# Layer 1's products of directly taken columns, made during layer 0, in a four-layer graph kernel

## The chip, the cores and the metric

The kernel runs on one core of a Trainium2 chip. The metric is the device time of one execution in microseconds (us). The kernel before the change took 1016.37 us (median of three runs, 1012.38 to 1018.28).

The engines are named as in the profile: PE is the matrix engine, PEld its weight loads, DVE the vector engine, ACT the scalar engine, POOL the engine that here issues the gathers by index, and SP the one that issues plain DMAs. [...]

## What is computed

There are N = 2708 nodes with D = 512 features, and a sparse weighted adjacency matrix `adj` with positive entries and a full diagonal. Four layers each replace `x` by `layernorm(x + layer(x, adj))`. The two that the change touches:

```python
# layer 0
adj_hat = adj + eye;  d = 1 / sqrt(adj_hat.sum(1))
layer0 = ((d[:, None] * adj_hat * d[None, :]) @ x) @ W.T + b
# layer 1
head = (adj > 0);  head = head / max(sqrt(sum(head * head, -1)), 1e-12)
inc  = adj + head
layer1 = (inc @ x) / sum(inc, -1)
```

Layer 1's incidence matrix depends on `adj` alone, so only its right factor, the rows of layer 0's result `x1`, has to be waited for. Layer 2 is an attention layer with gates, and layer 3 a product with signs; neither is touched.

## The kernel before

The node rows are cut into 22 blocks of 128 (block 21 has 20 rows). A prologue searches, for every block, which columns hold entries, and copies the needed pieces of the transposed adjacency into `packed[b]`: tiles of 128 columns by the block's rows. A block's tiles are of three kinds. **Direct tiles** (`direct(b)`, the table `DIRECT` at L34) are whole column blocks taken as they lie; for blocks 1 to 20 these are only column block 0, or 0 and 1, since the graph is densest there. Fifteen blocks have them: 1, 3, 5, 15 and 17 have two, ten others one, 20 tiles in all. **Gathered tiles** are 128 columns picked by a list; `ROOM` (L31) says how many, 98 over all blocks. Some of them are **narrow**: they concern only 32 or 64 of the block's rows. Block 0 is taken whole, a column block at a time.

Layer 0 (the loop at L1459) goes through the blocks in the order `sequence` = 0, 1, 21, 2, 3, ..., 20. For each block POOL issues one gather of 128 rows of `y_rows` per gathered tile (L613), PE multiplies tile by tile into a PSUM bank (L1369, in `add_tile`), DVE adds the result to the old rows (L1484), and the layer norm follows on DVE, with one square root on ACT (L642 to L683). The new rows stay in SBUF (`place_of_x(b)`) and are stored to `x1_rows` (L1488). Beside it runs `grow1` (L1421): block 0 of layer 1 needs all column blocks, and each block's part of it (two DVE operations for the incidence tile, one product on PE) is made two blocks after that block is finished. The table `between` hangs further steps on the places of the sequence: the counts and roots from which layer 1's row heads `head_row`, its scales `rdeg` and its diagonal factors `own1` come, for group n of the blocks at places 2 + 2n and 3 + 2n, and preparations of layers 2 and 3. At place 4 and after, head rows of the first group are therefore there.

Layer 1 (the loop at L1637) takes the blocks in the same order. It builds the incidence tiles on DVE (L1650, L1651), multiplies direct tiles first, then whole gathered tiles, then narrow ones (L1674, again by L1369), and in `finish1` ACT scales the block's own rows (L1562), DVE adds the scaled product (L1563), and the layer norm ends on ACT (L680). The gathers of layer 1 read `x1_rows` and so can't begin before layer 0's last rows are stored. PE also makes `project1` of the block before (four transposes L1588, a copy on ACT L1590, sixteen product records L1595) and `grow2` (L1628, L1629), the part of layer 2's block 0.

Within an engine the order of instructions isn't that of the source alone: a planner in the compiler's front end orders them by its own estimate of when each can run, and earlier source lines go first among the ready ones.

A product of a 128x128 tile by 128x512 values in float32 stands in the trace as two PE records, so "x2" is one tile.

Of the kernel before, what the change touches and what calls it, by code (L numbers as in the profile page):

```python
# [8 lines left out]
F32 = mybir.dt.float32  # L9
# [5 lines left out]
ALU = mybir.AluOpType  # L15
# [4 lines left out]
P = 128  # L20
# [487 lines left out]
def sparse_layers(ctx, tc, x, adj, adj_t, w0_t, b0, w_sa, a_sa, w_gcnb, b_gcnb, wa, ba, wb, bb, w3_t,  # L508
# [819 lines left out]
        t, spans = i - len(direct(b)), SPANS[SPLIT[b]]  # L1328
        return spans[t][1:] if 0 <= t < len(spans) else (0, rows(b))

    def whole_runs(b: int, most: int, apart: bool = False):

        nd, n = len(direct(b)), narrow(b)
        whole = [i for i in range(tiles(b)) if not nd <= i < nd + n]
        runs = []
        for i in whole:
            if runs and sum(runs[-1]) == i and runs[-1][1] < most and not (apart and i == nd + n):
                runs[-1] = (runs[-1][0], runs[-1][1] + 1)
            else:
                runs.append((i, 1))  # L1340
        return runs
# [31 lines left out]
    def last_of(b: int, i: int, order):  # L1373
# [3 lines left out]
            span(b, j)[1] <= r0 or span(b, j)[0] >= r1 for j in order[order.index(i) + 1 :]  # L1377
        )

    sum1 = ps_mm.tile([P, D], F32, tag="sum1", name="l1_0", bufs=1)  # L1380
    with tc.tile_pool(name="s_l0", bufs=10, reuse_waits="tile") as lp:


# [37 lines left out]
        def grow1(j: int):  # L1421

            r = rows(j)
            inc = lp.tile([P, P], F32, tag="inc0", name=f"inc0_{j}", bufs=2)
            a = packed[0][:r, j, :]
            nc.vector.scalar_tensor_tensor(
                inc[:r], a, 0.0, head0_row[0][:r], op0=ALU.is_gt, op1=ALU.mult
            )
            nc.vector.tensor_tensor(inc[:r], inc[:r], a, op=ALU.add)
            nc.tensor.matmul(  # L1430
                sum1, inc[:r], place_of_x(j)[:r, :D], start=(not grown1),
                stop=(len(grown1) == NB - 1),
            )
            grown1.append(j)

        between = {
            2: [attention_loads], 4: [lambda: attention_columns(0)],
# [21 lines left out]
        for at, b in enumerate(sequence):  # L1459
            m = rows(b)  # L1460
            old = place_of_x(b)
            nc.vector.tensor_tensor(old[:m, :D], old[:m, :D], b0_row[:m], op=ALU.add)
            if b:
                nd = len(direct(b))
                order_ = in_turns(b)
                src = {}
                for i in order_:
                    if i >= nd:
                        src[i] = gathered(lp, D, y_rows, b, i - nd)
                    else:  # L1470
# [12 lines left out]
            t = work.tile([P, D], F32, tag="t", name=f"t0_{b}")  # L1483
            nc.vector.scalar_tensor_tensor(  # L1484
                t[:m], ps[:m], dinv[:m, b : b + 1], old[:m, :D], op0=ALU.mult, op1=ALU.add
            )
            layernorm(old[:m, :D], t, m, f"0_{b}")
            nc.sync.dma_start(x1_rows[b * P : b * P + m, :], old[:m, :D])  # L1488
            for step_ in between.get(at, []):
                step_()  # L1490
        for b in sequence[-2:]:
            grow1(b)
    l0_ps.close()

    wp2 = w2.enter_context(tc.tile_pool(name="s_w22", bufs=1, side="right", reuse_waits="tile"))
# [62 lines left out]
    def finish1(b: int, ps):  # L1558
        m = rows(b)
        new, old = pairs.get(b, (f[b], f[b]))  # L1560
        t = work.tile([P, D], F32, tag="t", name=f"t1_{b}")
        nc.scalar.activation(t[:m], old[:m, :D], AF.Copy, scale=own1[:m, b : b + 1])  # L1562
        nc.vector.scalar_tensor_tensor(  # L1563
            t[:m], ps[:m], rdeg[:m, b : b + 1], t[:m], op0=ALU.mult, op1=ALU.add
        )
        layernorm(new[:m, :D], t, m, f"1_{b}", on_act=True)
        nc.sync.dma_start(x2_rows[b * P : b * P + m, :D], new[:m])

    with tc.tile_pool(name="s_l1", bufs=8, reuse_waits="tile") as lp:
# [67 lines left out]
        for at, b in enumerate(sequence):  # L1637
            m = rows(b)
            if b:
                nd = len(direct(b))  # L1640
                order_ = in_turns(b)
                src = {i: place_of_x(direct(b)[i]) for i in range(nd)}
                for i in order_:
                    if i >= nd:
                        src[i] = gathered(lp, D, x1_rows, b, i - nd)
                ps = ps_mm.tile([P, D], F32, tag="mm", name=f"l1_{b}")
                inc_of = {}

                def incidence(iv, a, row):
                    nc.vector.scalar_tensor_tensor(iv, a, 0.0, row, op0=ALU.is_gt, op1=ALU.mult)  # L1650
                    nc.vector.tensor_tensor(iv, iv, a, op=ALU.add)  # L1651

                for i0, n in whole_runs(b, 3):
                    inc = lp.tile([P, 3, P], F32, tag="inc0", name=f"inc{b}_{i0}", bufs=3)
                    iv = inc[:, :n, :m]
                    incidence(
# [549 lines left out]
```

## Time and profile before

| what | value |
|---|---|
| median of three runs | 1016.37 us (1012.38 to 1018.28) |
| the profiled execution's own time | 1015.66 us |
| its span, first to last instruction | 1013.9 us |
| PE busy over the span | 867.5 us (86%) |
| DVE / ACT / POOL busy | 654.6 / 381.2 / 513.0 us |
| mean granted PE clock | 0.924 |
| gathers of layer 0 (L613, y_rows) | 98, mean 995 ns |
| gathers of layer 1 (L613, x_rows) | 98, mean 967 ns |
| layer 1's direct products (L1369, `l<-f_other,inc`) | 40 records, 369.1 to 568.5 us |
| layer 0's main loop, after its first gathers | 224 to 361 us |
| change of layers | 361 to 400 us |
| layer 1, steady | 400 to 596 us |

The stage borders are read from the DVE operation that takes a block's product from PSUM: L1484 runs from 198.5 to 360.7 us, L1563 from 366.9 to 575 us. Busy time of an engine counts a record's whole length; PE's records overlap, so PE can be busy without being at its peak. "Remote" and "another core or an unknown queue" in a list of waits mean that the counter that was waited for was raised by nothing that the profile could name.

### The profile page before, as it was taken

Reading aid. Unit: us, or ns where it says so; the run is one execution under the profiler, and the core shown is the slowest. Engines: PE = TensorE matmul, PEld = TensorE weight load, DVE = VectorE, ACT = ScalarE, POOL = GpSimd, SP = SyncE. Lnnn points to the kernel's source line nnn. Section 1 sums busy time; section 2 is a strip of 40 time slices with the busy share of each in tenths; the row PEclk is TensorE's granted clock in tenths of the full one; section 3 lists DMA queues with packets and bytes.
Section 4 is the critical chain, followed back from the end, with each engine's and each line's share of the span. In section 5 each row is a group of like instructions: output and inputs, shape, how many; then the busy total and the mean of one; then the engine's idle time right before and its main releaser. Section 6 shows DMA issues by size and latency. Waiting matters only on the chain.

```text
span 1013.9 us, 12803 instructions
## 1 busy us (share of the span) xinstructions
PE 867.5 (86%) x3659; PEld 458.7 (45%) x3659; DVE 654.6 (65%) x2538; ACT 381.2 (38%) x822; POOL 513.0 (51%) x579
## 2 busy tenths in 40 slices
PE   1888889659587977989999988998999999699983
PEld 0444444212122324455555544453555555378762
DVE  5889797717366863546455436666888777556765
ACT  2665555100000012545445433333444333254654
POOL 2677888567666533646434034453454320066761
PEclk9898889879798988999999998999999999889986
DMA  9999895467676634766645266676786551299985
GB/s 288 332 330 313 293 299 162 142 197 215 189 228 202 199 122 132 216 198 207 199 150 165 80 235 239 225 272 219 261 320 224 176 176 44 82 308 331 310 233 169
DMA packets 93557, 220.06 MB, mean 217 GB/s; under 512 B 13660, under 2 KB 28364, under 8 KB 93476
## 3 DMA queue, kind: packets, MB, share of 16 engines
q0 software_dynamic: 43008, 127.61, 42.1%
q1 hardware_dynamic: 38520, 76.78, 22.3%
q10 hardware_dynamic: 11948, 14.76, 4.4%
q8 instruction: 31, 0.51, 0.2%
q14 instruction: 50, 0.41, 0.1%
HBM read 178.21 MB, written 31.71 MB: 207 GB/s over the span
## 4 chain that ended last, share of the span: by engine, by line
PE 63%; DVE 15%; issue 6%; DMA 6%; another core or an unknown queue 5%; ACT 3%; POOL 1%; ACTq 0%; DVEq 0%; SPq 0%; POOLq 0%
PE l L1369 11%; PE h L1595 7%; PE e L1820 6%; PE a L1820 6%; PE l L2075 4%; PE y L1106 4%; PE pg L1868 4%; PE l L2114 3%; PE pc L1868 3%; DMA xg<-x_rows,i 2%; PE e L1628 2%; PE px L1929 2%; PE a L1629 2%; DVE s_mask L874 1%
## 5 line engine op out<-in xcount | busy, mean ns | idle before, releaser
L613 POOL DMA_INDIRECT xg<-x_rows,i x98 | 94.8, 967 | 113.4 <-PE l L1369 65.7
L1072 POOL DMA_INDIRECT a<-in_adj_t_dram,row_at x98 | 111.0, 1132 | 59.2 <-DVE deg L817 24.0
L613 POOL DMA_INDIRECT xg<-y_rows,i x98 | 97.5, 995 | 50.3 <-issue 21.8
L1106 PE MATMUL y<-s_w,xt 128*128 128x512 f32 (+1 forms) x176 | 96.8, 702 | 0.0
L1369 PE MATMUL l<-xg,a 128*32 128x512 f32 (+3 forms) x196 | 83.2, 657 | 12.1 <-DMA xg<-y_rows,i 11.8
L613 POOL DMA_INDIRECT xg<-xw_rows,i x70 | 71.4, 1020 | 39.9 <-issue 16.5
L1796 POOL DMA_INDIRECT xg<-x_rows,i x60 | 59.9, 999 | 61.8 <-ACT ae L1551 18.0
L1595 PE MATMUL h<-s_wsa,xt 128*128 128x256 f32 (+3 forms) x352 | 83.5, 391 | 5.2 <-ACT xt L1590 5.0
L1796 POOL DMA_INDIRECT a<-x_rows,i x38 | 36.9, 970 | 93.3 <-DVE mask L1554 38.0
L1595 PEld LDWEIGHTS h<-s_wsa,xt 128*128 128x128 f32 (+1 forms) x352 | 65.4, 190 | 30.6 <-ACT xt L1590 14.0
L809 ACT ACTIVATE unused<-arow 128x1408 uint8<-128x1408 f32 (+3 forms) x44 | 58.3, 1325 | 2.4 <-DMA x_rows<-s_zero 1.7
L1106 PEld LDWEIGHTS y<-s_w,xt 128*128 128x128 f32 (+1 forms) x176 | 37.3, 223 | 43.4 <-issue 43.3
L2075 PE MATMUL l<-ws,pw 128*128 128x512 f32 (+1 forms) x210 | 52.0, 401 | 3.7 <-DVE pw L1999 3.7
L1820 PE MATMUL a<-xg,a 128*32 128x512 f32 (+2 forms) x120 | 50.9, 626 | 4.2 <-DMA xg<-x_rows,i 4.2
L1820 PE MATMUL e<-xg,ae 128*32 128x512 f32 (+2 forms) x120 | 47.9, 601 | 0.9 <-ACT ae L1556 0.9
L642 ACT ACTIVATE rsqs<-mv 128x1 f32<-128x1 f32 (+2 forms) x56 | 11.3, 201 | 94.8 <-DVE mv L671 48.9
L2075 PEld LDWEIGHTS l<-ws,pw 128*128 128x128 f32 (+1 forms) x210 | 40.4, 194 | 14.0 <-DVE pw L1999 4.6
L1868 PE MATMUL pg<-s_wg,pt 128*128 128x256 f32 (+1 forms) x176 | 44.9, 397 | 1.3 <-ACT pt L1856 1.3
L895 PE MATMUL find<-s_sides,s_mask 128*128 128x5 bf16 (+1 forms) x462 | 15.7, 166 | 34.8 <-DVE s_mask L891 25.0
L667 DVE BATCH_NORM_STATS2 st<-t 128x6 f32<-128x512 f32 (+1 forms) x66 | 45.3, 686 | 0.3
L1369 PEld LDWEIGHTS l<-xg,a 128*32 128x32 f32 (+3 forms) x196 | 19.6, 148 | 53.2 <-issue 33.0
L673 POOL TENSOR_TENSOR rs<-mv,s_neg_half 128x1 f32<-128x1 f32 (+1 forms) x22 | 12.9, 588 | 60.5 <-DVE mv L671 51.1
(306 smaller groups left out, 1965.6 us busy)
## 6 DMA issues: line engine op xcount, KB each, us to landing
arow<-in_adj_dram SPq DMA_DIRECT2D x21, 704.0 KB
arow<-in_adj_dram SPq DMA_DIRECT2D x21, 650.0 KB
x_rows<-f SPq DMA_DIRECT2D x40, 256.0 KB
aw<-in_adj_t_dram SPq DMA_DIRECT2D x21, 320.0 KB
y_rows<-yt ACTq DMA_DIRECT2D x20, 256.0 KB
x_rows<-h SPq DMA_DIRECT2D x19, 257.0 KB
f<-in_x_dram SPq DMA_DIRECT2D x19, 256.0 KB
h_own<-x_rows SPq DMA_DIRECT2D x19, 256.0 KB
```

The source lines that it names most:

```text
L613: nc.gpsimd.indirect_dma_start(out=t, out_offset=None, in_=src[:, :], in_offset=bass.IndirectOffsetOnAxis(ap=index[b][:, i : i + 1], axis=0),)
L667: nc.vector.bn_stats(st[:m], t[:m])
L809: nc.scalar.activation(unused[:m, : ar.shape[1]], ar, AF.Copy, accum_out=row_sums[:m, b, h : h + 1])
L1072: nc.gpsimd.indirect_dma_start(out=packed[b][:, t + len(direct(b)), :], out_offset=None, in_=adj_t, in_offset=bass.IndirectOffsetOnAxis(ap ...
L1106: nc.tensor.matmul(ps[:m], xt[:, k, :m], w0[:, k, :], start=(k == 0), stop=(k == KC - 1))
L1369: nc.tensor.matmul(ps[r0:r1], weights, moving, start=(i == order[0]), stop=last_of(b, i, order))
L1595: nc.tensor.matmul(ps, xt[:, k, :m], w[:, k, :], start=(k == 0), stop=(k == KC - 1))
L1796: nc.gpsimd.indirect_dma_start(out=g, out_offset=None, in_=x2_rows[:, :], in_offset=bass.IndirectOffsetOnAxis(ap=index[b][:, t : t + 1], a ...
L1820: nc.tensor.matmul(ps[r0:r1], weights, moving, start=(i == order[0]), stop=last_of(b, i, order))
L1868: nc.tensor.matmul(ps, pt[:, k, :m], w[:, k, :], start=(k == 0), stop=(k == KC - 1))
L2075: nc.tensor.matmul(whole[b], p[:r, h, b * P : (b + 1) * P], g[:r, :], start=(j == 0 and h == 0), stop=(j == NB - 1 and h == 1),)
L2114: nc.tensor.matmul(ps[:m], p[:, h, i * m : (i + 1) * m], src[i0 + i], start=False, stop=(i0 + i == len(src) - 1 and h == 1),)
```

## The change

The products of direct tiles leave layer 1's loop. A new function `begin1(b)` makes them in layer 0: two DVE operations for the incidence tiles, one product for each direct tile, ACT's scaling of the block's own rows, and one new DVE operation that adds the scaled product to them. The result stands where the block's rows of `x1` stood (`f[b]`; these have been stored by then, and block 0's product has used them). `begin1(b)` runs at the end of a place of the sequence, from two places after block b's own, and no earlier than place 4 + 2n of its group n. That puts block 1 at place 4; 2 and 3 at 6; 4 and 5 at 8; 7 at 10; 8 at 11; 9 at 12; 11 at 14; 13 at 16; 14 at 17; 15 at 18; 16 at 19; 17 at 20; and 20 after the loop. Its products use two PSUM banks in turn that are free at that time. Two small SBUF tiles of 1 KB a partition are added. Layer 1 then works only with gathered tiles, and `finish1` adds its product to what was begun.

```diff
-    def whole_runs(b: int, most: int, apart: bool = False):
+    def whole_runs(b: int, most: int, apart: bool = False, since: int = 0):
         nd, n = len(direct(b)), narrow(b)
-        whole = [i for i in range(tiles(b)) if not nd <= i < nd + n]
+        whole = [i for i in range(since, tiles(b)) if not nd <= i < nd + n]
...
+    def incidence(iv, a, row):
+        nc.vector.scalar_tensor_tensor(iv, a, 0.0, row, op0=ALU.is_gt, op1=ALU.mult)
+        nc.vector.tensor_tensor(iv, iv, a, op=ALU.add)
...
+        def begin1(b: int):
+            m, n = rows(b), len(direct(b))
+            inc = heads.tile([P, 2, P], F32, tag="incd", name=f"incd{b}", bufs=2)
+            iv = inc[:, :n, :m]
+            incidence(
+                iv, packed[b][:, :n, :],
+                head_row[:, None, b * P : b * P + m].to_broadcast([P, n, m]),
+            )
+            pool, tag = ((ps_mm, "sum0"), (ps_t, "t"))[len(begun) % 2]
+            ps = pool.tile([P, D], F32, tag=tag, name=f"l1d_{b}", bufs=1)
+            for i, j in enumerate(direct(b)):
+                nc.tensor.matmul(
+                    ps[:m], iv[:, i, :], place_of_x(j)[:, :D], start=(i == 0), stop=(i == n - 1)
+                )
+            nc.scalar.activation(
+                f[b][:m], place_of_x(b)[:m, :D], AF.Copy, scale=own1[:m, b : b + 1]
+            )
+            nc.vector.scalar_tensor_tensor(
+                f[b][:m], ps[:m], rdeg[:m, b : b + 1], f[b][:m], op0=ALU.mult, op1=ALU.add
+            )
+            begun.add(b)
+
+        to_begin = {}
+        for b in sorted(DIRECT):
+            n = GROUPS.index(group_of[b])
+            to_begin.setdefault(max(sequence.index(b) + 2, 4 + 2 * n), []).append(b)
...
             for step_ in between.get(at, []):
                 step_()
+            for c in to_begin.pop(at, []):
+                begin1(c)
         for b in sequence[-2:]:
             grow1(b)
+        for at in sorted(to_begin):
+            for c in to_begin[at]:
+                begin1(c)
...
-        nc.scalar.activation(t[:m], old[:m, :D], AF.Copy, scale=own1[:m, b : b + 1])
+        own = f[b] if b in begun else t
+        if b not in begun:
+            nc.scalar.activation(t[:m], old[:m, :D], AF.Copy, scale=own1[:m, b : b + 1])
         nc.vector.scalar_tensor_tensor(
-            t[:m], ps[:m], rdeg[:m, b : b + 1], t[:m], op0=ALU.mult, op1=ALU.add
+            t[:m], ps[:m], rdeg[:m, b : b + 1], own[:m, :D], op0=ALU.mult, op1=ALU.add
         )
...
-                order_ = in_turns(b)
-                src = {i: place_of_x(direct(b)[i]) for i in range(nd)}
-                for i in order_:
-                    if i >= nd:
-                        src[i] = gathered(lp, D, x1_rows, b, i - nd)
+                order_ = [i for i in in_turns(b) if i >= nd]
+                src = {i: gathered(lp, D, x1_rows, b, i - nd) for i in order_}
...
-                for i0, n in whole_runs(b, 3):
+                for i0, n in whole_runs(b, 3, since=nd):
```

More of the change, by code (lines that the diff above doesn't have):

```diff
@@ L1378, in last_of @@
         )
+    def incidence(iv, a, row):
+        nc.vector.scalar_tensor_tensor(iv, a, 0.0, row, op0=ALU.is_gt, op1=ALU.mult)
+        nc.vector.tensor_tensor(iv, iv, a, op=ALU.add)
     sum1 = ps_mm.tile([P, D], F32, tag="sum1", name="l1_0", bufs=1)
+    begun = set()
     with tc.tile_pool(name="s_l0", bufs=10, reuse_waits="tile") as lp:
@@ L1640, in sparse_layers @@
                 nd = len(direct(b))
-                order_ = in_turns(b)
-                src = {i: place_of_x(direct(b)[i]) for i in range(nd)}
-                for i in order_:
-                    if i >= nd:
-                        src[i] = gathered(lp, D, x1_rows, b, i - nd)
+                order_ = [i for i in in_turns(b) if i >= nd]
+                src = {i: gathered(lp, D, x1_rows, b, i - nd) for i in order_}
                 ps = ps_mm.tile([P, D], F32, tag="mm", name=f"l1_{b}")
                 inc_of = {}
-                def incidence(iv, a, row):
-                    nc.vector.scalar_tensor_tensor(iv, a, 0.0, row, op0=ALU.is_gt, op1=ALU.mult)
-                    nc.vector.tensor_tensor(iv, iv, a, op=ALU.add)
-                for i0, n in whole_runs(b, 3):
+                for i0, n in whole_runs(b, 3, since=nd):
                     inc = lp.tile([P, 3, P], F32, tag="inc0", name=f"inc{b}_{i0}", bufs=3)
```

## The prediction, made before the changed kernel was run

> **What bounds the kernel now.** The change moves work from layer 1 into layer 0, so I read first how full each engine is in each stage (the table by stretches: busy us and records of each engine, granted PE clock, DMA share).
>
> ```profile
> core 0: us, PE busy (x) PEld busy (x) DVE busy (x) ACT busy (x) POOL busy (x), PEclk, DMA share, GB/s
> 224.00:262.00 38.00, 29.68 (x91) 9.33 (x91) 22.26 (x96) 1.82 (x8) 27.34 (x27) 0.90 0.68 199
> 262.00:320.00 58.00, 44.78 (x150) 12.85 (x150) 32.40 (x144) 3.15 (x13) 38.02 (x39) 0.85 0.73 213
> 320.00:361.00 41.00, 40.06 (x131) 13.61 (x131) 35.08 (x167) 3.83 (x16) 16.99 (x17) 0.95 0.56 169
> 361.00:400.00 39.00, 27.22 (x64) 11.31 (x65) 18.46 (x74) 7.05 (x14) 16.41 (x17) 0.82 0.49 149
> 400.00:596.00 196.00, 190.19 (x725) 106.31 (x724) 99.45 (x388) 94.23 (x161) 80.25 (x83) 0.99 0.55 168
> ```
>
> Layer 1 (400 to 596) is PE's: busy 190 of 196 us, DVE and ACT half idle. But layer 0 isn't a stage with an idle PE either. Only its first part has room (PE 74.5 of 96 us up to 320); from 320 to 361 PE is busy for 40.1 of 41 us, with DVE at 35.1 close behind it. The chain of waits in that last part confirms it, with nothing but products in it:
>
> ```profile
> 346.10 0.97 PE l L1430 x2
> 347.07 1.86 PE l L1369 x4
> 348.93 1.06 PE l L1430 x2
> 349.99 2.06 PE l L1369 x4
> ```
>
> By engine, the chain's pieces add up to 39.9 us PE of 41 here; in 262 to 320 to 22.0 PE, 18.7 DVE and 12.7 "another core or an unknown queue" (DVE waiting for PE's counter); in 224 to 262 mostly to gathers and unnamed waits (PE 8.7 of 38).
>
> Last, PE's timeline in layer 1, for what a direct product costs there and what stands around it:
>
> ```profile
> 473.31 0.66 PE L1588 MATMUL xt1p<-s_ident,f 128*128 128x128 f32 x4
> 473.81 1.02 PE L1369 MATMUL l<-xg,inc 128*128 128x512 f32 x2
> 474.67 3.73 PE L1595 MATMUL h<-s_wsa,xt 128*128 128x256 f32 x16
> ...
> 522.96 0.60 PE L1588 MATMUL xt1p<-s_ident,f 128*128 128x128 f32 x4
> 523.39 1.88 PE L1369 MATMUL l<-f_other,inc 128*128 128x512 f32 x4
> 525.11 3.64 PE L1595 MATMUL h<-s_wsa,xt 128*128 128x256 f32 x16
> ```
>
> Starts are what count: 523.39 to 525.11 is 1.72 us for two direct tiles, 0.86 us each. They also fill the wait between the transposes (L1588) and the products that need ACT's copy of them (L1595). Block 10 (at 473.81) has no direct tile, and there one gathered tile fills that wait as well, without a gap. The gathered rows are early: POOL waits for PE to free its buffers, not the reverse.
>
> ```profile
> POOL xg L613 <- PE l L1369: 57.6, 20, 7.3
> ```
>
> [...] the granted clock is 0.82 at the change of layers and 0.99 in layer 1. [...] The trace has 749 ns from start to end for L1563, and the next DVE operation begins 0.67 us after its start, where DVE is full.
>
> **The change part by part.**
>
> *Layer 1, removed PE work.* Of the 40 direct records, 34 (17 tiles) lie after 400 us, where PE decides: 17 x 0.86 = 14.6 us saved. Block 2's one tile (396.68) stands on the chain for 1.71 us, at half clock: 1.7 saved. Block 1's two tiles (369.09) are worth nothing: PE goes on to wait for the first gathers, which were issued only at 368.58 and are used from 372.63. The filling of the wait at L1595 is kept, since every block has a whole gathered tile left. For the gathers of the early blocks (eight, six, six, five and six in blocks 2 to 6, 1.25 us each in POOL's queue, against about 10 us a block) I give 1.0 back. Layer 1: **-15.3**. At worst -12 (gathers decide in blocks 2 to 6), at best -16.3.
>
> *Layer 1, removed side work.* ACT loses 15 scalings (0.72 each), DVE the 30 incidence operations of direct tiles. Both engines are half idle: 0, and what hides it is PE's 190 us. If gathers decided instead, it would still be 0.
>
> *Layer 0, added products.* They come singly between other groups. The same is true of `grow1` (L1430), whose tile takes 0.97 to 1.06 us in the chain above; I take 1.0. Block 1 (place 4, near 240 us) falls where gathers are waited for: of 2 tiles I count 0.3 us. Blocks 2, 3, 4, 5, 7, 8, 9 (places 6 to 12; L1484 of these places runs at 262.7 to 306.7) have 9 tiles, 9.0 us. PE or the wait for PE's counter holds 34.7 of 58 us of the chain, but part of that counter wait is a hole that they can fill: half, 4.5. Blocks 11, 13, 14, 15, 16, 17 (places 14 to 20, 325 to 361 us) have 8 tiles, and there PE is full: 8.0. Block 20's tile comes after the loop, when PE waits for layer norms and gathers (361 to 372): 0. PE's sum **12.8**; bounds 7 (only half the late tiles count) and 19 (all count).
>
> *Layer 0, added DVE work.* Per begun block two incidence operations (next start after about 0.2 us each, as L1426 and L1429 show; a second tile adds some 0.13 each) and the new add from PSUM, 0.67: 15 x 1.07 + 5 x 0.26 = 17.3 us. In 262 to 320, seven blocks, some 8 us, DVE has 18.7/58 of the chain: 2.5. In 320 to 361, six blocks: DVE goes from 35.1 to 42, PE from 40 to 48, so DVE still isn't the bound; for two engines so full in lockstep I add 1.0. Block 20's operations lie beside the layer norm that the first gathers wait for: 0.5. DVE's sum **4.0**, between 1 and 12.
>
> *Added ACT work.* 15 x 0.72 = 10.8 us on an engine that is busy for 8.8 of 137 us: 0 by itself. But the copy waits for `grow1`'s product and for the store of the block's rows (SP, L1488), both from two places earlier or the same place, and behind it in ACT's queue stand the square roots (L642) of the layer norms; the new DVE add waits for it and for the product, and the next block's L1484 may stand behind that. This is the lower rival. No DMA is added or moved past another: the stores and gathers keep their number and order on SP and POOL. Two more SBUF tiles shift the buffers by 2 KB a partition; 0, at most 1 either way.
>
> *Sum.* -15.3 + 12.8 + 4.0 = **+1.5 us** on the profiled execution's 1015.66 (span 1013.9 and 1.8 around it): 1017.2. That execution lies 0.7 below the median 1016.37 of the runs shown, so for a median I say **1018**.
>
> **The rivals.** *(A) The move is even*, as summed: 1018. Chance 0.42. For it: PE is full on both sides of the move, and the same 20 products are made. *(B) Layer 0's holes take more*: PE isn't busy for 21 us before 320, and in 361 to 372 it works half the time; if the planner's order puts the products there, PE's sum falls to 7 and DVE's to 1, and with -16.3 the result is -8.3: 1008. Chance 0.27. Against it: in those holes DVE also stands still (one of its waits for PE's counter takes 9.2 us), and the products need DVE's incidence tiles first. *(C) DVE's order decides late layer 0*: the new add waits in DVE's queue for PE and ACT, with the layer norm of the next block behind it, so that PE in turn waits for DVE. If each of 13 blocks stalls DVE for 0.7 us more than its own work, that is 9 more: +10.5, 1027. It decides as soon as DVE's time for a begun block in 320 to 361 (35.1 us for ten blocks, 3.5, and 4.7 with the new work) passes PE's (4.1, and 5.1 with one tile); the margin is 0.4 us, and a single wait for PE and ACT can use it up. Chance 0.31. That the products aren't moved in effect (planned behind the loop) is within B: they would then lie in the change of layers.
>
> **How the numbers follow.** A measurement of this kernel tells about 0.5% from no change, 5.1 us: 1011.3 to 1021.5. Taking A as same, B as faster, C as slower: 0.27, 0.42, 0.31. A's own range is 1012 to 1023 (layer 1 at -12 is within it). To leave out no more than 2 in 10, the range reaches into both others: below to 1006, where B's bounds meet (7 + 1 - 16.3, with another 2 for shifted waits), above to 1028, C's value and a little over.
>
> **What would show it.** Right: layer 1's steady stretch shortens by 14 to 16 us with PE still over 95% busy, no `l<-f_other,inc` record after the change of layers, and layer 0 grows by 15 to 18 us, about 9 of it after block 11's L1484. B: layer 0 grows by under 10. C: in late layer 0 DVE over 95% busy or waiting for PE and ACT at the new add, with PE's busy share falling below 0.9. Wrong altogether: layer 1 shortening by less than 10 us, which would mean that gathers or ACT's copy take PE's place as its bound.

## The result, and the profile after

Side by side in the first comparison, 22 runs each, the changed kernel has a median of 1017.1 us and the kernel before one of 1011.9 us: a ratio of 1.0068, 95% interval 1.0041 to 1.0094. The forecast of 1018 lies 0.9 us off, but partly by luck: the kernel before came out 4.5 us below the median that the forecast started from. The change itself is 5.2 us by the two medians; the ratio, which leaves out slow runs (over 1.5% above the fastest of their kernel), says 0.68%, some 7 us. The sum had +1.5.

The same two kernels were compared again beside the experiments below. There the kernel before took 960.1 us and the changed one 959.0: ratio 0.9990, interval 0.9976 to 1.0003. So the answer isn't one number. In the profiled execution of the changed kernel the mean granted PE clock is 0.952 there and 0.932 in the first comparison. Whether the chip is the cause isn't shown: the experiments' record names three chips, on which the kernel before took 959.7, 960.2 and 960.1 us, and none for the first comparison. Both traces are needed.

First the changed kernel's trace from the first comparison (profiled execution 1021.69 us, span 1020.0; before 1015.66 and 1013.9). This is the table by stretches, with borders at the same blocks as in the prediction, so the stretches have other lengths.

```profile
core 0: us, PE busy (x) PEld busy (x) DVE busy (x) ACT busy (x) POOL busy (x), PEclk, DMA share, GB/s
...
256.00:329.00 73.00, 50.24 (x185) 17.05 (x182) 40.70 (x165) 7.59 (x19) 45.36 (x45) 0.81 0.65 193
329.00:377.00 48.00, 45.91 (x133) 15.79 (x134) 39.80 (x178) 7.43 (x21) 15.42 (x16) 0.96 0.44 138
...
414.00:604.00 190.00, 177.02 (x678) 98.94 (x677) 92.76 (x359) 84.46 (x147) 79.42 (x83) 0.98 0.57 173
```

Layer 0's last addition (L1484 before, L1517 now) moved from 360.7 to 377.2 us: layer 0 grew by 16.5. From there to the end of layer 1's last project1 it took 227.7 us before and 219.4 now: layer 1 shrank by 8.3 only. Layers 2 and 3 are 2.2 shorter. PE is busy for 177 of 190 us in steady layer 1, 93% where it had been 97%. The growth of layer 0 isn't where it was forecast: 13.6 us of it come before block 11's addition, 2.9 after it. The chain of waits there is again made of products, with a few pieces of the new addition (L1459) in it:

```profile
342.19 0.98 PE l1d L1453 x2
343.17 0.02 issue
343.19 0.75 DVE f L1459
343.94 0.07 DVE hd L1186
344.01 0.21 DVE inc L1434
```

A begun product (l1d) takes 0.98, as estimated, but then PE waits: the DVE addition of 0.75 stands in DVE's queue ahead of the incidence tile that the next grow1 product needs.

In layer 1, PE's gaps before the h products (now L1635) are what replaces the direct tiles. One of four, from the timeline:

```profile
477.32 0.60 PE L1628 MATMUL xt1p<-s_ident,f 128*128 128x128 f32 x4
477.46 0.81 ACT L680 ACTIVATE f<-t,rs 128x512 f32<-128x512 f32 x1 [1.06 <-issue]
477.76 1.02 PE L1369 MATMUL l<-xg,inc 128*128 128x512 f32 x2
481.02 0.59 ACT L1630 COPY xt<-xt1p 128x512 f32<-128x512 f32 x1 [2.75 <-remote]
481.07 0.29 DVE L1381 SCALAR_TENSOR_TENSOR inc<-a,s_head_row 128x128 f32<-128x128 f32 x1 [3.64 <-remote]
481.30 0.94 POOL L613 DMA_INDIRECT xg<-x_rows,i  x1 [1.91 <-remote]
481.66 1.57 PE L1635 MATMUL h<-s_wsa,xt 128*128 128x256 f32 x5 [2.88 <-ACT xt L1630]
```

The transposes' last record ends at 477.92. ACT's copy of them is free to run at 478.27, when ACT has finished L680, and runs at 481.02. DVE and POOL wait at the same time, for a counter that the trace doesn't name, and are let go within 0.3 us of it. What all three wait for is PE's work (in the kernel before, at 486.5 us, the same three engines are let go within 0.35 us of each other, and the trace names PE for all of them). So it isn't ACT that is late, nor one product: PE's counter as a whole is seen 3 us after PE's records. Over steady layer 1 the rows of the waits say how often:

```profile
PE h L1635 <- ACT xt L1630: 9.3, 3, 3.5
POOL xg L613 <- PE l L1369: 54.0, 25, 6.1
```

The columns are total us, times and the longest. The page lists 12.0 us of idle PE time ahead of L1635, in four gaps (429.5, 450.1, 478.8 and 499.0); in the kernel before there were two, 5.0 us. POOL still waits mostly for PE.

### The profile page after: what moved, and what is told of

It reads as the page before. It is cut to its first block, busy times and chain, and to the rows that moved or that the text cites. A ratio compares the mean times of both kernels' runs of the same rounds, so it can differ in the third digit from the quotient of the medians.

```text
span 1020.0 us, 12829 instructions
## 1 busy us (share of the span) xinstructions
PE 861.6 (84%) x3659; PEld 458.0 (45%) x3659; DVE 663.9 (65%) x2553; ACT 380.6 (37%) x822; POOL 511.9 (50%) x579
## 4 chain that ended last, share of the span: by engine, by line
PE 63%; DVE 12%; issue 9%; DMA 7%; ACT 4%; another core or an unknown queue 3%; POOL 2%; ACTq 0%; DVEq 0%; SPq 0%; POOLq 0%
PE l L1369 10%; PE h L1635 7%; PE e L1853 6%; PE a L1853 6%; PE l L2108 4%; PE y L1106 4%; PE pg L1901 3%; PE l L2147 3%; PE pc L1901 3%; DMA xg<-x_rows,i 3%; PE l1d L1453 2%; PE px L1962 2%; PE l L1435 2%; PE a L1669 2%
## 5 line engine op out<-in xcount | busy, mean ns | idle before, releaser
L1072 POOL DMA_INDIRECT a<-in_adj_t_dram,row_at x98 | 109.3, 1115 | 61.6 <-DVE deg L817 25.7
L613 POOL DMA_INDIRECT xg<-y_rows,i x98 | 99.7, 1017 | 58.0 <-PE l L1369 29.8
L1635 PE MATMUL h<-s_wsa,xt 128*128 128x256 f32 (+3 forms) x352 | 85.3, 397 | 12.0 <-ACT xt L1630 9.3
L1106 PE MATMUL y<-s_w,xt 128*128 128x512 f32 (+1 forms) x176 | 92.9, 677 | 1.9 <-ACT xt L1098 1.9
L1369 PE MATMUL l<-xg,a 128*32 128x512 f32 (+3 forms) x196 | 77.4, 671 | 12.7 <-DMA xg<-y_rows,i 12.7
L1635 PEld LDWEIGHTS h<-s_wsa,xt 128*128 128x128 f32 (+1 forms) x352 | 66.2, 192 | 38.0 <-ACT xt L1630 19.6
L1829 POOL DMA_INDIRECT a<-x_rows,i x38 | 37.0, 973 | 87.4 <-DVE mask L1592 34.6
L667 DVE BATCH_NORM_STATS2 st<-t 128x6 f32<-128x512 f32 (+1 forms) x66 | 45.3, 686 | 0.3
L1642 DVE COPY h<-h 128x260 f32<-128x260 f32 (+1 forms) x20 | 8.6, 428 | 52.8 <-PE h L1635 39.8
```

The costliest lines, as they stand in the source:

```text
L613: nc.gpsimd.indirect_dma_start(out=t, out_offset=None, in_=src[:, :], in_offset=bass.IndirectOffsetOnAxis(ap=index[b][:, i : i + 1], axis=0),)
L667: nc.vector.bn_stats(st[:m], t[:m])
L1072: nc.gpsimd.indirect_dma_start(out=packed[b][:, t + len(direct(b)), :], out_offset=None, in_=adj_t, in_offset=bass.IndirectOffsetOnAxis(ap ...
L1106: nc.tensor.matmul(ps[:m], xt[:, k, :m], w0[:, k, :], start=(k == 0), stop=(k == KC - 1))
L1369: nc.tensor.matmul(ps[r0:r1], weights, moving, start=(i == order[0]), stop=last_of(b, i, order))
L1635: nc.tensor.matmul(ps, xt[:, k, :m], w[:, k, :], start=(k == 0), stop=(k == KC - 1))
```

## The experiments

They ran in three sets, each beside the kernel before (959.7 to 960.2 us). The microseconds beside a ratio are what it lies above or below 1, times 960. "Layer 0's end" is the last addition of layer 0, "layer 1" the time from there to the last h product. The traces differ by up to 4 us before anything of the change is reached; the column "block 1 to x1" is free of that. It runs from block 1's addition in layer 0 to the first gather of `x1`.

| run | ratio to before (95%) | us | layer 0's end | block 1 to x1 | layer 1 |
|---|---|---|---|---|---|
| l1_alone | 0.9908 (0.9879 to 0.9938) | -8.8 | 332.3 | 130.8 | 201.5 |
| l0_alone | 1.0156 (1.0127 to 1.0184) | +15.0 | 344.8 | 141.9 | 213.4 |
| after_shift | 0.9914 (0.9889 to 0.9940) | -8.3 | 342.4 | 140.6 | 194.6 |
| before_shift | 0.9945 (0.9924 to 0.9966) | -5.3 | 334.0 | 130.6 | 207.6 |
| begin_early | 1.0029 (1.0013 to 1.0044) | +2.8 | 332.8 | 131.7 | 211.8 |
| begin_late | 1.0032 (1.0016 to 1.0048) | +3.1 | 343.8 | 141.9 | 205.6 |
| products_only | 0.9936 (0.9915 to 0.9957) | -6.1 | 336.6 | 133.3 | 200.9 |
| sides_only | 0.9993 (0.9979 to 1.0008) | -0.7 | 344.7 | 142.2 | 199.0 |
| act_takes | 0.9927 (0.9902 to 0.9953) | -7.0 | 338.6 | 136.7 | 199.8 |
| act_takes_shift | 0.9887 (0.9861 to 0.9913) | -10.8 | 336.0 | 135.2 | 193.8 |
| no_early_gathers | 0.9849 (0.9821 to 0.9877) | -14.5 | 331.8 | 130.6 | 198.2 |
| after_again | 0.9990 (0.9976 to 1.0003) | -1.0 | 342.3 | 140.1 | 200.2 |

No trace of the kernel before was taken in these sets. Its layer 0 is that of l1_alone, no_early_gathers and before_shift (ends at 331.8 to 334.0, block 1 to x1 130.6 to 130.8), and its layer 1 is that of l0_alone (213.4).

### The two halves apart

l1_alone begins nothing in layer 0 and leaves the direct tiles out of layer 1:

```diff
-            for c in to_begin.pop(at, []):
-                begin1(c)
...
-        for at in sorted(to_begin):
-            for c in to_begin[at]:
-                begin1(c)
```

> Half of the change: layer 1 without its direct tiles, and nothing begun in layer 0. It leaves the products of the direct tiles out altogether. Theory F (the direct tiles stood as a filler ahead of a wait: after the transposes PE waits for ACT's copy before the products of project1, and PE's counter is now and then seen some 3 us late; with less between the two, more of that lateness shows): layer 1 gives only about half of what was summed, 7 to 10 us against the kernel before, with gaps before the h products of about 8 to 12 us in all. Rival S (the sum for layer 1 holds, and the four gaps in the one trace of the changed kernel are that execution's own): 14 to 16 us faster.

l0_alone is the kernel before, with begin1 added to its layer 0 and its result put into spare tiles:

```diff
...
+            two = heads.tile([P, D], F32, tag="two", name=f"two{b}", bufs=2)
+            nc.scalar.activation(
+                two[:m], place_of_x(b)[:m, :D], AF.Copy, scale=own1[:m, b : b + 1]
+            )
+            nc.vector.scalar_tensor_tensor(
+                two[:m], ps[:m], rdeg[:m, b : b + 1], two[:m], op0=ALU.mult, op1=ALU.add
+            )
...
```

> The other half: layer 0 with all twenty begun products, ACT scalings and DVE additions, written to two spare tiles that nobody reads, and layer 1 as before. Theory F: layer 0 costs what was summed, so 15 to 18 us slower than the kernel before, nearly all of it ahead of layer 1's first block. Rival S, which has to explain the same total of 5 to 7 us: layer 0 costs more than was summed, 20 to 23 us.

Measured: -8.8 and +15.0. Both numbers are theory F's and not S's, yet the reason given for the first isn't what the trace shows: l1_alone has no PE gap over 0.8 us from 369.6 us to the end of layer 1. What it has is longer products. Layer 1's record groups from block 2's addition to block 20's, each counted from its start to the next record's start:

| us | l0_alone (direct tiles in layer 1) | l1_alone | after_again |
|---|---|---|---|
| direct | 14.9 | 0 | 0 |
| narrow gathered | 22.0 | 26.8 | 24.7 |
| whole gathered | 21.7 | 22.0 | 22.2 |
| h, transposes, grow2 | 101.7 | 101.4 | 101.9 |
| all, with gaps | 160.5 | 150.7 | 149.0 |

The 34 direct records were worth the 14.9 us that the prediction's 17 x 0.86 said; 2.7 to 4.8 of them come back at the narrow tiles. All of that in after_again, and 3.8 of the 4.8 in l1_alone, lies in blocks 3 to 6, that is between block 2's addition and block 6's. The row of the narrow products over these blocks, from the groups by shape, first with direct tiles (l0_alone), then without (l1_alone):

```profile
L1369 PE MATMUL l<-xg,incn 128*32 128x512 f32 x32 | 4.3, 605 | 0.0
```

```profile
L1369 PE MATMUL l<-xg,incn 128*32 128x512 f32 x32 | 8.0, 605 | 0.2 <-DMA xg<-x_rows,i 0.2
```

The mean length of one record is the same in both, 605 ns; the time in which any of them runs, the number behind the bar, goes from 4.3 to 8.0 us. In the kernel before, the four narrow tiles of a block took 1.06 us when all were there (441.60 us, eight records), and a single one 1.04 (380.92, two records), both at full clock, so the four take longer when they come one by one. In l1_alone's blocks 3 to 6 POOL never waits for longer than 0.3 us at a time: it issues without a pause, and PE waits for it. With direct tiles, in l0_alone, POOL still waits there for PE to free its buffers, up to 3.2 us at a time. First l0_alone, then l1_alone:

```profile
POOL xg L613 <- PE l L1369: 7.1, 5, 3.2
```

```profile
POOL xg L613 <- PE l L1369: 1.2, 4, 0.3
PEld l L1369 <- DMA xg<-x_rows,i: 3.1, 5, 1.1
```

### Which gathers decide

no_early_gathers is l1_alone with the narrow tiles of blocks 2 to 6 taken from SBUF:

```diff
-                src = {i: gathered(lp, D, x1_rows, b, i - nd) for i in order_}
+                src = {
+                    i: place_of_x(0) if 2 <= b <= 6 and i < nd + narrow(b)
+                    else gathered(lp, D, x1_rows, b, i - nd) for i in order_
+                }
```

> Layer 1 alone (no direct products in layer 1, nothing begun in layer 0), and for blocks 2 to 6 the narrow tiles are taken from the rows of block 0 in SBUF in place of gathered ones, so that 20 gathers fall away there; the direct products are left out and these narrow products are wrong by that. Theory G (in blocks 2 to 6 the saved products are lost again in waits for gathers, most of them at the narrow tiles: 7.8 us for 32 records with no direct tiles against 4.0 with them): 3 to 6 us faster than layer 1 alone (0.9908), so -12 to -15 us against before, with narrow records at about 4 us in these blocks. Rival (the narrow tiles are slower for another reason, such as their incidence tiles on DVE): within 2 us of layer 1 alone, -11 to -7 us.

Measured: 0.9849, 5.7 us below l1_alone. Blocks 3 to 6 take 31.4 us and not 34.6, and the narrow records are shorter again, at 5.3 us for the 4 that were expected:

```profile
L1369 PE MATMUL l<-f_other,incn 128*32 128x512 f32 x32 | 5.3, 605 | 0.0
```

That is theory G: without the gathers in front of them, the same products lose most of their waits, while DVE makes their incidence tiles as before, so the rival falls. The rest of the 5.7 isn't placed (the trace differs by 2.7 us in the whole span, 3.2 of it in these blocks, and the medians of these two runs are known to some 3 us each).

### Early blocks against late ones

begin_early and begin_late begin only some of the blocks; the others keep their direct tiles in layer 1:

```diff
+    def soon(b: int):
+        return b <= 5
...
-        for b in sorted(DIRECT):
+        for b in sorted(b_ for b_ in DIRECT if soon(b_)):
...
-                order_ = [i for i in in_turns(b) if i >= nd]
+                since = nd if b in begun else 0
+                order_ = [i for i in in_turns(b) if i >= since]
```

In begin_late the condition is b > 5.

> The change for blocks 1 to 5 alone (eight of the twenty direct tiles, at places 4 to 8); the other ten blocks keep their direct tiles in layer 1. Theory G (in layer 1's first blocks the gathers set the pace once the direct tiles are gone, so the early ones save little there, and in layer 0 before block 9 they cost next to nothing): layer 0 plus 0 to 2 us, layer 1 minus 1 to 3, together -3 to +1 us against the kernel before. Rival P (each tile saves and costs the same wherever it lies, 0.45 us saved and 0.75 paid): +2.4 us.

> The change for blocks 7 to 20 alone (twelve tiles, at places 10 to 20 and after the loop). Theory G: nearly the whole price is here, layer 0 plus 11 to 14 us, and layer 1 minus 8 to 10 (12 x 0.86 = 10.3 less a little), together +2 to +6 us against the kernel before. Rival P: +3.7 us with layer 0 plus 9 and layer 1 minus 5.4. The two are told apart by the stages in the trace more than by the total.

The totals, +2.8 and +3.1, fit rival P better than G: P said +2.4 and +3.7, and begin_early lies above G's +1. The stages decide between them. begin_early: layer 0's end at 332.8 (0.5 later than in l1_alone), and in layer 1 from block 2 to block 20 161.3 us, where l0_alone with all its direct tiles has 160.5. Five tiles fewer there, and no gain: 4.6 us of direct records are gone and the narrow ones are longer by 5.5. begin_late: layer 0's end at 343.8, 11.5 later than in l1_alone, and 151.2 us from block 2 to block 20, 9.3 less for twelve tiles. P wanted 5.4. So the places that are free in layer 0 give nothing in layer 1, and those that give in layer 1 cost in layer 0. begin_early's +2.8 doesn't lie in these stages.

What isn't understood: the two parts add up to +5.9 us, the halves of the change to +6.2, and the whole change beside these experiments gives -1.0. In part the pieces aren't pure (l0_alone keeps ACT's scaling in layer 1, and its first gather of x1 is 2.5 us later than in the whole change); the order of all later instructions is planned anew for each kernel, and in begin_early and begin_late layers 2 and 3, which no run alters, take 415.1 and 416.5 us against 412.8 to 414.3 in l0_alone, l1_alone and after_again (411.3 to 417.5 over all runs of the table). Differences of some 3 us between such parts are not to be trusted.

### What layer 0 pays for

products_only makes the incidence tiles and products in layer 0 (it chooses the PSUM bank by the block's number and not by turns), sides_only everything but the products:

```diff
-            pool, tag = ((ps_mm, "sum0"), (ps_t, "t"))[len(begun) % 2]
+            pool, tag = ((ps_mm, "sum0"), (ps_t, "t"))[b % 2]
...
-            nc.scalar.activation(
-                f[b][:m], place_of_x(b)[:m, :D], AF.Copy, scale=own1[:m, b : b + 1]
-            )
-            nc.vector.scalar_tensor_tensor(
-                f[b][:m], ps[:m], rdeg[:m, b : b + 1], f[b][:m], op0=ALU.mult, op1=ALU.add
-            )
-            begun.add(b)
+            end = lp.tile([P, 1], F32, tag="end", name=f"end{b}", bufs=2)
+            nc.vector.tensor_copy(end[:m], ps[:m, :1])
```

```diff
-            pool, tag = ((ps_mm, "sum0"), (ps_t, "t"))[len(begun) % 2]
-            ps = pool.tile([P, D], F32, tag=tag, name=f"l1d_{b}", bufs=1)
-            for i, j in enumerate(direct(b)):
-                nc.tensor.matmul(
-                    ps[:m], iv[:, i, :], place_of_x(j)[:, :D], start=(i == 0), stop=(i == n - 1)
-                )
...
-                f[b][:m], ps[:m], rdeg[:m, b : b + 1], f[b][:m], op0=ALU.mult, op1=ALU.add
+                f[b][:m], place_of_x(0)[:m, :D], rdeg[:m, b : b + 1], f[b][:m],
+                op0=ALU.mult, op1=ALU.add
```

> What in layer 0 costs: incidence tiles and products are made there as in the change, and a DVE copy of one column reads each product so that it has a reader; ACT's scaling and the full DVE addition are left out, and so is the products' share of the result (layer 1 makes the scaling as before and has no direct tiles). Against layer 1 alone (0.9908 of the kernel before, -9 us): if PE's own time is the price, as the prediction's sum has it (12.8 of 16.8), 11 to 13 us slower than that, so +2 to +4 us against before. If DVE's order is (rival C of the prediction), only 4 to 7 us slower than layer 1 alone, -5 to -2 us against before.

> The counterpart: in layer 0 the incidence tiles, ACT's scaling and the DVE addition are made as in the change, with the addition reading rows of block 0 in SBUF in place of the product; the twenty products are left out, and so is their share of the result. Against layer 1 alone (-9 us): if PE's own time is the price, 2 to 5 us slower than that, so -7 to -4 us against before. If DVE's order is, 8 to 11 us slower, -1 to +2 us.

Against l1_alone, whose layer 0 is that of before, the products with their incidence tiles cost 2.7 us (from block 1 to x1 2.5 more), the side work without products 8.2 (11.4 more). The 2.7 is less than even the DVE theory's 4 to 7; each of the two is known to some 3 us. The prediction's sum had it the other way round. The two don't add up: from block 1 to x1 the whole change takes 9.3 more than l1_alone, 2.1 less than the side work without the products, so beside the side work the products cost nothing.

Where the products cost is to be seen at block 11's addition. From block 1's addition up to it products_only is 1.2 us shorter than l1_alone; from there to the last addition it takes 53.7 us in place of 48.9. So the late part does pay for its products, 4.8 us for nine tiles (the prediction had 8.0 for eight), and the part before it pays nothing.

In sides_only the chain of waits of the last 12 us of layer 0 is DVE and nothing else; some of its pieces:

```profile
333.21 0.66 DVE f L1453
...
334.93 0.66 DVE t L1512
...
338.44 0.75 DVE f L1453
...
344.75 0.66 DVE t L1512
```

L1453 is the addition here, L1512 the addition of layer 0's own products. They don't wait; they stand in line. In the whole change (after_again, layer 0) 15 additions have 11.1 us of their own and only 1.3 us of waiting ahead of them:

```profile
L1459 DVE SCALAR_TENSOR_TENSOR f<-l1d,s_rdeg,f 128x512 f32<-128x512 f32 x15 | 11.1, 741 | 1.3 <-PE l1d L1453 1.1
```

Most of this is hidden behind PE until the last blocks. There the chain of waits of the whole change goes through the additions (L1459), with layer 0's own addition (L1517) and the last layer norm (L667) behind them:

```profile
338.69 0.75 DVE f L1459
339.44 0.05 DVE s_own L1205
339.49 0.66 DVE t L1517
...
343.48 0.75 DVE f L1459
344.23 0.06 DVE rsqs L661
344.29 0.60 DVE st L667
```

PE's last gathered product of layer 0 ends 2.7 us before DVE begins the last addition in after_again, and 0.1 us or less before it in l1_alone and products_only.

### ACT in place of DVE

act_takes removes that addition from layer 0. ACT alone takes the product out of PSUM, and the block's own rows are loaded again in layer 1:

```diff
-            nc.scalar.activation(
-                f[b][:m], place_of_x(b)[:m, :D], AF.Copy, scale=own1[:m, b : b + 1]
-            )
-            nc.vector.scalar_tensor_tensor(
-                f[b][:m], ps[:m], rdeg[:m, b : b + 1], f[b][:m], op0=ALU.mult, op1=ALU.add
-            )
+            nc.scalar.activation(f[b][:m], ps[:m], AF.Copy, scale=rdeg[:m, b : b + 1])
...
+        old = again.get(b, old)
+        nc.scalar.activation(t[:m], old[:m, :D], AF.Copy, scale=own1[:m, b : b + 1])
+        if b in begun:
+            nc.vector.tensor_tensor(t[:m], t[:m], f[b][:m], op=ALU.add)
...
+                if b in begun and b not in pairs:
+                    again[b] = work.tile([P, D], F32, tag="xb", name=f"x1_{b}")
+                    nc.sync.dma_start(again[b][:m], x1_rows[b * P : b * P + m, :])
```

> The changed kernel with the new DVE addition taken out of layer 0: there ACT alone takes each begun product from PSUM, scaled, into the place of x1; layer 1 loads the block's own rows again from memory by SP (not for block 1, whose rows are still held), scales them on ACT as the kernel before does, and adds the begun product with one more DVE operation. Theory D (the DVE time of the addition, 15 x 0.67 = 10 us, is the main price in layer 0): 8 to 11 us faster than the changed kernel (1.0068 of before), that is -5 to -1 us against before. Rival R (what hurts is that ACT's queue waits for PE, with the square roots of the layer norms behind): ACT still waits, so +3 us or more against before.

Measured: -7.0 us, below the expected range of -5 to -1, and 6.2 below after_again (medians 952.8 and 959.0). Layer 0's end comes at 338.6 in place of 342.3 and the first gather of x1 at 345.5 in place of 350.9, with the same products; but 2.0 us of this lead stand already at block 1's addition, ahead of everything begun, and from block 1 to x1 the gain is 3.4. PE's last gathered product of layer 0 ends 0.1 us ahead of the last addition again. Layer 1 is no longer than in after_again (199.8 and 200.2). ACT waits longer than in the change (41.0 us before its 15 operations, against 35.3), so waiting on ACT isn't what was saved:

```profile
L1457 ACT ACTIVATE f<-l1d,s_rdeg 128x512 f32<-128x512 f32 x15 | 10.3, 687 | 41.0 <-PE l1d L1454 39.4 <-DMA x_rows<-f 1.5
```

Theory D holds in kind and R, which asked for +3 us or more, falls, but the addition is worth less than the 8 to 11 us expected, and how much isn't sharp. The same step in the kernels with the cut of the next section, from after_shift to act_takes_shift, gives 2.6 us by the ratios and 5.4 from block 1 to x1. So it is 3 to 6 us. What remains isn't PE's alone: act_takes needs 5.9 more than l1_alone from block 1 to x1, products_only 2.5; the 3.4 between them, for ACT's part, aren't explained.

### The products of project1 one block later

The products of project1 were put one block later than its transposes and ACT's copy, in both kernels and in act_takes (the cut also lets grow2 and the start of layer 2's first sums come a block later, which wasn't tried apart):

```diff
...
             nc.scalar.copy(xt[:, :, :m], pt[:, :, :m])
+            xts[j] = xt
+
+        def project1b(j: int):
+
+            m, xt = rows(j), xts.pop(j)
...
+            if at > 1:
+                project1b(sequence[at - 2])
             if at:
                 project1(sequence[at - 1])
```

> The changed kernel with project1 cut in two: the transposes and ACT's copy of a block stay where they are, its sixteen products come one block later, so that three to four gathered tiles stand between the copy and the products on PE. Theory F: the gaps before the h products go (12 us in the trace of the changed kernel), of which perhaps a third comes back at other places and at the end, so 5 to 9 us faster than the changed kernel (1017.1), that is 1008 to 1012, and level with the kernel before. Rival L (PE itself really runs late at these places, and its records are only ahead of it): the gaps vanish from the records and the time doesn't move by more than 2 us, 1015 to 1019.

> The same cut of project1 in the kernel before, which had 5 us of such gaps in its trace and direct tiles besides to fill them. Theory F: 1 to 4 us faster than before, less than the same cut gives the changed kernel. Rival L: no change, within 2 us.

> The same with project1 cut in two (its products one block later), which made the changed kernel -0.9% of before. Theory D: another 8 to 11 us off, -15 to -20 us against before. Rival R: -8 us, as with the cut alone.

Measured: -8.3, -5.3 and -10.8 us against before. Compared with the same kernel without the cut, that is -7.3 for the changed kernel (0.9914 to 0.9990), -5.3 for the kernel before (1 to 4 were expected) and -3.8 for act_takes. The cut helps everywhere; the differences between the three are within their intervals of 2 to 4 us, and by the traces layer 1, from the first gather of x1, gains 5.6, 5.1 (against l0_alone) and 6.1. But these traces can't judge F against L, since the gaps before the h products that F wanted to close aren't there in this set in the first place. What the cut does here is seen in the groups from block 2 to block 20: narrow records 22.4 us in place of 24.7, h records 63.7 in place of 65.3. act_takes_shift, expected at -15 to -20, missed its range by 4 us. It is still the fastest version that leaves nothing out, ahead of both kernels: 948.4 us.

### The change once more

> The changed kernel itself beside these. If the two halves add up as measured (0.9908 and 1.0156), the ratio to before is 1.003 to 1.010. Its trace tells whether the waits for ACT's copy ahead of the h products (12 us in the first trace of the changed kernel, none over 0.8 us in that of layer 1 alone) belong to the change or to that execution.

Measured: 0.9990, 0.4% under the lower end that I expected from the halves. Its table by stretches (again the same blocks as borders):

```profile
core 0: us, PE busy (x) PEld busy (x) DVE busy (x) ACT busy (x) POOL busy (x), PEclk, DMA share, GB/s
...
243.00:288.00 45.00, 42.92 (x161) 14.02 (x160) 33.55 (x141) 6.18 (x16) 34.44 (x35) 1.00 0.79 248
288.00:342.00 54.00, 51.35 (x164) 17.65 (x163) 46.43 (x202) 8.84 (x24) 25.99 (x26) 1.00 0.57 177
...
380.00:529.00 149.00, 148.55 (x587) 82.69 (x586) 81.27 (x316) 73.47 (x126) 75.22 (x79) 1.00 0.65 200
```

From 204 to 342 us PE has no gap longer than 1.3 us, and it is busy for 148.5 of 149 us in steady layer 1, at full clock. Layer 0 ends 10.0 us later than in l1_alone; layer 1 takes 13.2 us less than with its direct tiles (200.2 and 213.4). None of the four gaps is there. So the change by itself doesn't bring them; they go with the executions of the first comparison.

## Why the prediction was right or wrong

**The total.** Case A, the even move, is what the second comparison shows (-1.0 us, within its 0.5%); the first lies just outside of it, at +0.68%, with an interval from 0.41 to 0.94. The stated time of 1018 is near in the first, but the sum of +1.5 is 4 to 5 us short there.

**Layer 1's removed PE work, 17 x 0.86 = 14.6.** Right as a term: the group measures 14.9. Its correction for the gathers of blocks 2 to 6, 1.0, was too small: the narrow tiles cost 2.7 in the whole change and 4.8 in l1_alone, most of it there, and begin_early shows the early blocks to gain nothing at all. "At worst -12 (gathers decide in blocks 2 to 6)" was the right mechanism; layer 1 came to -13.2 in the second comparison, inside the bounds, though the steady part, from block 2's addition to block 20's, shortens by 11.5 and not by the 14 to 16 given as a sign of being right. The prediction saw POOL waiting for PE over all of layer 1 and took that for all of its blocks; the total hides that at its start POOL runs without pause.

**"The filling of the wait at L1595 is kept, since every block has a whole gathered tile left."** Right in the second comparison, wrong in the first: one tile of 0.86 us covers the wait when PE's counter is seen promptly, and doesn't cover 3 us. The page of the kernel before already had 5.0 us of such waits ahead of L1595, with direct tiles in place. In the first comparison such waits are 7.0 us longer than in the kernel before, against layer 1's shortening, which came to -8.3. The stated test "layer 1 shortening by less than 10 us" came out there, though not for the cause that it named: neither gathers nor ACT's copy took PE's place; PE's counter was seen late. That the four gaps rather than two are owed to the missing direct tiles is only argued: tiles in that place shorten such a gap, but the gap at 485 us in the kernel before had a direct and a gathered tile in front of it and still lasted 2.0 us.

**Layer 0's PE, 12.8, and DVE, 4.0.** This is the step that failed. That its sum (16.8) met the first trace's 16.5 was luck: 13.6 of these came before block 11's addition, with PE idle for 3 to 9 us at a time, and the second comparison has 10.0. Measured apart, PE's products with their incidence tiles cost 2.7 us by the times and 2.5 from block 1 to x1, below the term's lower bound of 7; the DVE addition alone costs 3 to 6. The 4.5 for the nine tiles before block 11 came to nothing. The reading "there PE is full: 8.0" was right in kind, since the late part pays 4.8 in products_only, but too large: busy records at 40.1 of 41 us were no proof of a PE without room. With 20 products more, the other products' groups shrink: from block 7's addition to the first gather of x1, products_only spends 14.2 us on l1d and 6.7 fewer on gathered tiles than l1_alone. That the gathered products had stretched over waits for their tiles, as the narrow ones do in layer 1, is the likely reason; it isn't shown for layer 0. DVE was put at "so DVE still isn't the bound" and block 20's operations at 0.5. At the end of layer 0 it is the bound: there DVE stands in line with nothing to spare, and 0.75 us of an addition ahead of the last layer norms are 0.75 us more until the first gather.

**The rivals.** C named the right engine for a part of the price (the new addition in DVE's queue) but not its way: DVE waits only 1.3 us at the addition, it is the addition's own time. B named what happened to PE's products: of 20 at some 0.95 us, 19 us, only 2.5 were left at the first gather of x1. Together they give nearly A's number, so that A's total came out without A's reason, which was that PE is full on both sides.

**Where "about 9 of it after block 11's L1484" was tested.** In the first comparison it was 2.9, in the second 5.3 (block 11's addition 4.7 us later and the last one 10.0 later than in l1_alone): less than the forecast both times. products_only has 4.8 of it.

**What stays open.** Why the change costs 0.68% in one comparison and nothing in the other. The traces of the first show PE idle for 2 to 10 us at a time, in both kernels, mostly while DVE waits for a counter that the trace doesn't name. In layer 0's main part the holes of over 2 us add up to the same, 25.8 us before and 25.7 after, so the change doesn't have more of them there. Half clock does last longer in it (30.7 us from 261 to 333, against 24.0 from 259 to 324), which is worth at most half of the 6.7 us between the two, by an estimate from one direct tile in the kernel before: 1.71 us at a granted clock of 0.50 (396.88 us), 0.86 at full clock (523.39). In layer 1 the gaps before h are 7.0 us more, but one at the change of layers (5.9 us at 387.7 before, 2.1 at 407.1 after) is 3.8 less. Each of these rests on one trace of each kernel, and the sum doesn't account for all of the 11 us by which the two comparisons differ in the stages (16.5 and 10.0 in layer 0, 8.3 and 13.2 in layer 1). Whether the late counter comes from the chip or from something in the executions wasn't tried. Nor do the traces tell whether the counter is late or PE itself, whose records have modelled ends (rival L).

## What to carry to other kernels

Moving work from a full engine pays only where that engine is what is late: look block by block at what fills its buffers (here POOL's gathers), since the totals of a stage hide that its first blocks wait for them (begin_early took 4.6 us of direct records out, and the narrow ones grew by 5.5). A busy share near 1 doesn't say that an engine has no room (late layer 0 had PE busy for 40.1 of 41 us, and nine tiles more, of some 0.95 us each, cost 4.8 there); leaving the products out, or adding only them, tells. And of what is moved, count the small engine's share too, above all where a stage ends and the next one waits: one DVE operation of 0.74 us a block in a chain of layer norms cost no less than one or two products of 0.86 us a block on PE, and giving it to an engine that idles (ACT) took 3 to 6 us off.

## What the runs showed of the hardware that wasn't expected

PE's counter was seen late, against the ends of PE's records, which are modelled. In the first comparison's traces, ACT, DVE and POOL were let go within 0.3 us of one another 3 us after PE's records had ended (481.02, 481.07 and 481.30 us, records ended 477.92 and 478.8). In layer 0 of the changed kernel the longest such wait is 10.1 us:

```profile
310.33 0.49 DVE L1164 TENSOR_SCALAR pos<-a 128x640 bf16<-128x640 f32 x1 [10.12 <-remote]
...
310.88 0.29 PE L1166 MATMUL hr<-valid,pos 128*128 128x1 bf16 x5 [8.73 <-DVE rsqs L661]
```

PE stood still for 8.7 us there (302.15 to 310.88), and the granted clock was 0.50 from 305.2 to 315.4 us, from 3 us after PE's last record until 4.5 us after its next one. The begun tile at 313.17 us, at 0.50, takes 1.84 us to the next product's start; the one at 317.99 us, at full clock, takes 1.06. In the second comparison nothing of the kind is in the changed kernel's trace from 204 us to the end of layer 1, and the kernel as a whole is 58 us faster (959.0 and 1017.1), with the same instructions.
